# The messages of a graph layer by Strassen's product, four groups left out

## The chip, the cores and the metric

The kernel runs on one core of a Trainium2 chip. The core has a matrix engine (TensorE, PE in the profile; PEld is its loading of weights), a vector engine (VectorE, DVE), a scalar engine (ScalarE, ACT), a general engine (GpSimd, POOL) and an engine that issues most transfers (SyncE, SP). They work side by side, each on its own queue in order, and wait for one another by semaphores. TensorE writes its results to PSUM, eight banks of 128 x 512 fp32 numbers; the other engines read them from there into SBUF. The metric is the device time of one execution in microseconds (us).

## The reference: two layers on 128 graphs

The input is `x`, 128 graphs of 128 nodes with 256 features, and a sparse adjacency for each. Layer 0 mixes two projections by a gate and normalises. Layer 1, which the change touches, computes per graph (all in fp32):

```python
msg = relu(x @ w_msg.T + b_msg)                    # 128 nodes x 256
A = exp(-dist)                                     # from 3 coordinates per node
x_nmp = A @ msg                                    # over the nodes
x_in = concatenate([x_conv, x_nmp])                # x_conv: two convolutions over the nodes
gi = x_in @ w_ih.T + b_ih                          # 128 x 768
gh = x @ w_hh.T + b_hh                             # 128 x 768
r, z = sigmoid(gi_r + gh_r), sigmoid(gi_z + gh_z)
out = (1 - z) * tanh(gi_n + r * gh_n) + z * x
x = layernorm(x + out)
```

The second layer's adjacency multiplies `A` in the code in place of the mask (L974). The product of the change is the one in the first line: 128 nodes x 256 features by 256 x 256 weights, for each graph.

## The kernel before, in words

The work has three stages: layer 0 with the start of layer 1 over 64 pairs of graphs (to about 670 us), the convolution in the frequency domain (to 848 us), and a loop over 32 groups of G = 4 graphs for all the rest (848 us to the end). The change lies in the third stage.

What one group `g` goes through there:

- `load_c`, `load_x1`, `load_y` read its `x1T` (features on partitions, 256 x 512 nodes), adjacency, `x1` and convolution coefficients by SP's queue, two groups ahead.
- `l1_project(g)` makes the sums of `x1T` on POOL (`l1_sums`, tile `sh`) and the messages: for each pair of graphs a PSUM bank, in it for each graph two matmuls of 128 x 128 weights by 256 columns (L927). DVE adds the bias (L931, 128 x 512), ACT applies the relu (L935). Groups 2 and 3 (`EARLY`) got their messages in the first stage and only read them back.
- `l1_own`, `l1_kernel` make the distances of two groups at once in the tile `acc`, which holds four whole banks; ACT takes the exponential (L970), DVE multiplies the adjacency (L974).
- `l1_synth(d)` is the way back of the convolution for two groups, also in the four banks of `acc` (L891, L898); DVE adds `x1T` (L908), ACT applies the relu (L911), POOL makes the sums `sc`.
- `l1_gather(g)` multiplies `A` by the messages (`nmp_ps`, L983, eight matmuls of 128 columns); ACT copies (L987), DVE makes the sums `sm`.
- `l1_gru(g, pr)`, for each of the two pairs of graphs, makes the gates by Strassen's product in Winograd's form: the pair of graphs and the two halves of the features make a 2 x 2 block matrix, the weights another, and seven products take the place of eight. Each product is three matmuls of 384 columns (`g_ps`, L1050) into one bank of the pool `psC`, which has four banks, taken in turn. DVE adds the products up (L1063 to L1067, L1085, L1086) and so empties the banks; two of the additions are on POOL (L1083, L1084). `l1_update` finishes the gates (L1009 to L1025) and the norm (L308, L309, POOL's L192 and L193, L316, L318).

The left factors of a Strassen product are blocks of the input and four sums of them. `l1_sums` makes the four: s1 (L997), s2 (L998), s3 (L999), s4 (L1000), for `x1T` in `sh`, for the convolution in `sc`, for the gathered messages in `sm`. The right factors are blocks of the weights and four differences, made once in `l1_factors`.

TensorE's order in the loop is written out by hand: gather of `g`, messages of `g + 1`, first gates of `g`, and after odd `g` the way back of the next two groups, then second gates of `g`; after odd `g` the distances of the next two groups stand between the fourth and the fifth product of the second gates. A planner orders the other engines from the order of the program and the costs that it assumes. So three things are in turn in `acc` (and, with the change, four), and the four banks of `psC` go round among everything else.

An "even group" below is an even `g`, whose gather is followed by the messages of `g + 1`; before it TensorE had the distances, after an odd one comes the way back.

Of the kernel before, what the change touches and what calls it, by code (L numbers as in the profile page):

```python
# [9 lines left out]
F32 = mybir.dt.float32  # L10
I32 = mybir.dt.int32
AF = mybir.ActivationFunctionType
ALU = mybir.AluOpType

P = 128
D = 256
NC = D // P
J = 2
G = 4
# [15 lines left out]
def gnn_layers_kernel(ctx: ExitStack, tc: tile.TileContext, a: dict, out: bass.AP):  # L35
# [10 lines left out]
    nc = tc.nc  # L46
# [30 lines left out]
    w_msg = const.tile([P, NC, D], F32, tag="w_msg", name="w_msg")  # L77
    b_msg = const.tile([P, D], F32, tag="b_msg", name="b_msg")
# [244 lines left out]
    def nodes(q):  # L323
        return slice(q * P, (q + 1) * P)
# [366 lines left out]
    def cpool(name, bufs, stack=cctx, **kw):  # L691
        return stack.enter_context(tc.tile_pool(name=name, bufs=bufs, reuse_waits="tile", **kw))
# [91 lines left out]
    with tc.manual_schedule(engines={E.Activation, E.Pool}):  # L784
        for k in range(M // 2):
# [4 lines left out]
            for blk in range(2):  # L790
                for c in range(NC):
                    nc.tensor.matmul(  # L792
                        py[:, blk, :], lhsT=coefs(blk if k == 0 else 2 * k + 1 - blk, c),
                        rhs=w[:, blk, c, :], start=(c == 0), stop=(c == NC - 1),
# [3 lines left out]
            else:  # L798
# [5 lines left out]
                for c in range(NC):  # L804
                    nc.tensor.matmul(  # L805
                        pz[:, 0, :], lhsT=hs[:, c, :], rhs=ws[:, c, :],
                        start=(c == 0), stop=(c == NC - 1),
# [15 lines left out]
    ck = cpool("ck", 2)  # L823
    acc = cpool("acc", 1, space=PSUM)
    psc = cpool("psC", 4, space=PSUM)

    def bankc(name):
        return psc.tile([P, 512], F32, tag="ps", name=name)

    cs = cpool("cs", 1)  # L830
    factors = {}

    def l1_factors():

        for kind, w in (("h", w_hh), ("c", w_ih[:, 0:NC]), ("m", w_ih[:, NC : 2 * NC])):
            t = cs.tile([P, 4, 3 * P], F32, tag=f"t{kind}", name=f"t_{kind}")
            b11, b12, b21, b22 = (w[:, c, h, :] for c in range(NC) for h in range(2))
            nc.vector.tensor_sub(t[:, 0, :], b12, b11)
            nc.vector.tensor_sub(t[:, 1, :], b22, t[:, 0, :])
            nc.vector.tensor_sub(t[:, 2, :], b22, b12)  # L840
            nc.vector.tensor_sub(t[:, 3, :], t[:, 1, :], b21)
            factors[kind] = (b11, b21, b22, t[:, 3, :], t[:, 0, :], t[:, 1, :], t[:, 2, :])

    def load_c(g):
        s = st[g] = {}
        s["x1T"] = wb.tile([P, NC, 2, D], F32, tag="w", name=f"cx1T_{g}").rearrange("p c r o -> p c (r o)")
        for r in range(2):
            nc.sync.dma_start(s["x1T"][:, :, r * J * P : (r + 1) * J * P], x1T_d[2 * g + r])
        s["adjT"] = ci.tile([P, G, P], F32, tag="adjT", name=f"cadjT_{g}")
        nc.sync.dma_start(s["adjT"], adjT[:, g * G : (g + 1) * G, :])  # L850

    def load_x1(g):
        s = st[g]
        if g in EARLY:
            s["msg"] = ck.tile([P, G, D], F32, tag="msg", name=f"msg_{g}")
            for r in range(2):
                nc.sync.dma_start(
                    s["msg"][:, r * J : (r + 1) * J, :].rearrange("p j e -> p (j e)"),
                    msg_d[EP.index(2 * g + r)],
                )  # L860
        s["x1"] = ci.tile([P, G, D], F32, tag="x1", name=f"cx1_{g}")
        nc.sync.dma_start(
            s["x1"], x1_d[2 * g : 2 * g + 2].rearrange("r j n e -> n (r j) e")
        )
# [3 lines left out]
    def load_y(d):  # L868

        yl = cy.tile([P, P], F32, tag="yl", bufs=2, name=f"yl_{d}")  # L870
        for e in range(2):
            g = 2 * d + e
            yt = cy.tile([P, G, D], F32, tag="yt", name=f"yt_{g}")
            nc.sync.dma_start(yt, y_d[g * G : (g + 1) * G, 0:P, :].rearrange("q m f -> m q f"))
            for c in range(NC):
                r = NC * e + c
                nc.sync.dma_start(
                    yl[32 * r : 32 * r + 32],
                    y_d[g * G : (g + 1) * G, P:M, c * P : (c + 1) * P],
                )  # L880
            sy[g] = yt, yl


    def l1_synth(d):
        four = acc.tile([P, 4, 512], F32, tag="acc", name=f"conv2_ps_{d}")
        pcs = {}
        for e in range(2):
            for c in range(NC):
                pc = pcs[e, c] = four[:, NC * e + c, :]
                for q in range(G):  # L890
                    nc.tensor.matmul(  # L891
                        pc[:, nodes(q)], lhsT=sy[2 * d + e][0][:, q, c * P : (c + 1) * P], rhs=S,
                        start=(q == 0), stop=False, skip_group_check=True,
                    )
        for e in range(2):
            for c in range(NC):
                k = slice(32 * (NC * e + c), 32 * (NC * e + c) + 32)
                nc.tensor.matmul(  # L898
                    pcs[e, c], lhsT=sy[2 * d + e][1][k, :],
                    rhs=SLb[k].rearrange("p q n -> p (q n)"),  # L900
                    start=False, stop=True, skip_group_check=True,
                )
        for e in range(2):
            s = st[2 * d + e]
            s["xcT"] = ck.tile([P, NC, G * P], F32, tag="xcT", bufs=3, name=f"xcT_{2 * d + e}")
            for c in range(NC):
                dst = s["xcT"][:, c, :]
                nc.vector.scalar_tensor_tensor(  # L908
                    dst, pcs[e, c], scale2[:, c : c + 1], s["x1T"][:, c, :], ALU.mult, ALU.add
                )  # L910
                nc.scalar.activation(dst, dst, AF.Relu, bias=shift2[:, c : c + 1])  # L911
            l1_sums(2 * d + e, "c", s["xcT"], nc.gpsimd)


    def l1_project(g):
        s = st[g]
        x1T = s["x1T"]
        l1_sums(g, "h", x1T, nc.gpsimd)
        if g in EARLY:
            return  # L920
        msg = ck.tile([P, G, D], F32, tag="msg", name=f"msg_{g}")
        for pr in range(G // 2):
            pm = bankc(f"msg_ps_{g}_{pr}")
            for j in range(2):
                q = 2 * pr + j
                for c in range(NC):
                    nc.tensor.matmul(  # L927
                        pm[:, j * D : (j + 1) * D], lhsT=x1T[:, c, nodes(q)], rhs=w_msg[:, c, :],
                        start=(c == 0), stop=(c == NC - 1),
                    )  # L930
            nc.vector.tensor_tensor(  # L931
                msg[:, 2 * pr : 2 * pr + 2, :], pm.rearrange("p (j e) -> p j e", j=2),
                b_msg.unsqueeze(1).to_broadcast([P, 2, D]), ALU.add,
            )
        nc.scalar.activation(msg, msg, AF.Relu)  # L935
        s["msg"] = msg

# [53 lines left out]
    def l1_sums(g, kind, src, engine):  # L991

        v = src.rearrange("p c (r j n) -> p c r j n", r=G // 2, j=2)
        a11, a12, a21, a22 = (v[:, c, :, j, :] for j in range(2) for c in range(NC))
        t = ck.tile([P, 4, G // 2, P], F32, tag=f"s{kind}", name=f"s{kind}_{g}")
        s1, s2, s3, s4 = (t[:, i] for i in range(4))
        engine.tensor_tensor(s1, a21, a22, ALU.add)  # L997
        engine.tensor_tensor(s2, s1, a11, ALU.subtract)  # L998
        engine.tensor_tensor(s3, a11, a21, ALU.subtract)  # L999
        engine.tensor_tensor(s4, a12, s2, ALU.subtract)  # L1000
        st[g][f"f{kind}"] = (a11, a12, s4, a22, s1, s2, s3)
# [91 lines left out]
    with tc.manual_schedule(engines={mybir.EngineType.PE}):  # L1093
        load_c(0)
        load_c(1)
        load_y(0)
        for g in range(2):
            load_x1(g)
            l1_own(g)
        l1_project(0)  # L1100
        l1_kernel(0, 1)
        l1_project(1)
        l1_factors()
        l1_synth(0)
        for g in range(NG):
            d = g // 2
            if g + 2 < NG:
                load_c(g + 2)
                if g % 2 == 0:
                    load_y(d + 1)  # L1110
                load_x1(g + 2)
                l1_own(g + 2)
            l1_gather(g)
            if 2 <= g + 1 < NG:
                l1_project(g + 1)
            l1_gru(g, 0)
            if g % 2 == 1 and d + 1 < ND:
                l1_synth(d + 1)
            if g + 1 < NG:

                l1_gru(g, 1, {4: lambda: l1_kernel(g + 1, g + 2)} if g % 2 == 1 else {})
# [44 lines left out]
```

## Time and profile before

| | |
|---|---|
| time, median of 3 runs | 1989.94 us (1989.74 to 1992.71) |
| profiled execution, its own time | 1989.79 us |
| its span, first to last instruction | 1988.0 us |
| PE busy | 1948.1 us (98%) |
| PEld busy | 1322.5 us (67%) |
| DVE busy | 1452.2 us (73%) |
| ACT busy | 743.2 us (37%) |
| POOL busy | 701.0 us (35%) |
| messages on PE (L927), 480 instructions | 108.7 us |
| gates on PE (L1050) as a share of the chain that ended last | 43% |

An instruction's row shows its start, its duration, engine, line, what it writes and reads, and, in brackets, how long the engine had idled before it and for whom. Durations of successive instructions overlap, so the distance from start to start says what one costs its engine. A matmul of fp32 counts as two instructions. The third stage repeats itself every two groups, 70.36 us (`nmp_ps` of groups 18 and 20 start at 1484.68 and 1555.04).

### The profile page before, as it was taken

The numbers are of one execution on the slowest core, as the hardware profiler recorded it, in microseconds if no ns is written. First come the engines' busy times: TensorE is split into PE (matmuls) and PEld (weight loads), VectorE is DVE, ScalarE is ACT, GpSimd is POOL, SyncE is SP. The second block draws the span as 40 slices with busy tenths as digits, with TensorE's granted clock in tenths as the row PEclk, the third lists the DMA queues.
The fourth block names the chain that finished last, engine by engine and source line by source line (L and its number), as shares of the span: only waits on it lengthen the run. The fifth ranks groups of instructions, "written<-read, shape, count | busy, mean of one in ns | idle before, by whom it ended". The sixth has DMA issues, their size and how long they took to land.

```text
span 1988.0 us, 26049 instructions
## 1 busy us (share of the span) xinstructions
PE 1948.1 (98%) x8203; PEld 1322.5 (67%) x8203; DVE 1452.2 (73%) x2866; ACT 743.2 (37%) x1489; POOL 701.0 (35%) x983
## 2 busy tenths in 40 slices
PE   8999999999999999999999999999999999999996
PEld 5666666666666788866666666666666666666663
DVE  7788888888888544477677767777776776767775
ACT  3666666666665311122222222222232222222221
POOL 3223232232322355543333424323342433333331
PEclk9999999999999999999999999999999999999998
DMA  5787877777776799962212221221221222121100
GB/s 148 213 240 211 240 211 230 236 225 221 230 223 195 265 316 334 315 205 82 81 48 68 78 71 59 81 67 62 66 81 57 72 76 64 57 79 54 37 12 22
DMA packets 328687, 279.87 MB, mean 141 GB/s; under 512 B 150885, under 2 KB 268909, under 8 KB 328550
## 3 DMA queue, kind: packets, MB, share of 16 engines
q1 hardware_dynamic: 317622, 264.32, 43.1%
q0 software_dynamic: 4224, 8.37, 1.6%
q10 hardware_dynamic: 6704, 5.52, 0.9%
q8 instruction: 67, 1.10, 0.2%
q14 instruction: 70, 0.57, 0.1%
HBM read 173.26 MB, written 104.86 MB: 140 GB/s over the span
## 4 chain that ended last, share of the span: by engine, by line
PE 64%; DVE 1%; DMA 0%; issue 0%; ACT 0%; POOL 0%; POOLq 0%; ACTq 0%; SPq 0%; DVEq 0%
PE g_ps L1050 43%; PE y_ps L792 5%; PE msg_ps L927 5%; PE nmp_ps L983 3%; PE conv_ps L891 3%; PE z_ps L805 3%; PE conv_ps L898 1%; PE dist_ps L964 1%; DMA wb<-w_d 0%; ACT o L1009 0%; DVE hs L802 0%; PE turn_ps L943 0%; DVE coords L725 0%; DVE o L1019 0%; DVE left L727 0%
## 5 line engine op out<-in xcount | busy, mean ns | idle before, releaser
L353 PE MATMUL f_ps<-w,xT 128*128 128x512 f32 x512 | 246.2, 603 | 8.5 <-DVE xT L423 6.9
L192 POOL TENSOR_SCALAR rstd_b<-mv_b 128x2 f32<-128x2 f32 (+1 forms) x65 | 12.5, 192 | 529.8 <-DVE mv_b L309 529.8
L1009 ACT ACTIVATE o<-o 128x1024 f32<-128x1024 f32 (+1 forms) x65 | 67.8, 1044 | 268.8 <-DVE o L1086 264.8
L353 PEld LDWEIGHTS f_ps<-w,xT 128*128 128x128 f32 x512 | 89.5, 190 | 110.2 <-issue 77.7
L1050 PE MATMUL g_ps<-t_h,sh 128*128 128x384 f32 x384 | 156.8, 490 | 0.0
L1050 PE MATMUL g_ps<-t_c,sc 128*128 128x384 f32 x384 | 155.2, 486 | 0.0
L1050 PE MATMUL g_ps<-t_m,sm 128*128 128x384 f32 x384 | 155.2, 486 | 0.0
L318 ACT ACTIVATE y<-y,nb_b,rstd_b 128x256 f32<-128x256 f32 x128 | 70.0, 593 | 219.0 <-DVE nb_b L316 219.0
L358 PEld LDWEIGHTS gate_ps<-w,xT 128*128 128x128 f32 x512 | 97.4, 190 | 68.1 <-issue 53.9
L1083 POOL TENSOR_TENSOR u<-u,p 128x512 f32<-128x512 f32 x63 | 79.8, 1267 | 162.6 <-DVE p L1067 162.6
L358 PE MATMUL gate_ps<-w,xT 128*128 128x256 f32 x512 | 131.4, 379 | 0.0
L792 PE MATMUL y_ps<-wb,H 128*128 128x256 f32 x544 | 128.4, 379 | 0.8 <-POOL ws L800 0.8
L445 PE MATMUL conv_ps<-conv_w,x1T 128*128 128x259 f32 x512 | 122.8, 382 | 5.5 <-DVE x1T L423 3.7
L800 POOL TENSOR_TENSOR ws<-wb 128x512 f32<-128x512 f32 x67 | 93.3, 1392 | 91.9 <-PE z_ps L805 54.7
L192 POOL TENSOR_SCALAR rstd_a<-mv_a 128x2 f32<-128x2 f32 x64 | 12.2, 191 | 299.9 <-DVE mv_a L309 238.9
L362 ACT ACTIVATE hom<-f_ps,norm 128x256 f32<-128x256 f32 x128 | 60.6, 473 | 145.7 <-PE f_ps L353 139.2
L792 PEld LDWEIGHTS y_ps<-wb,H 128*128 128x128 f32 x544 | 103.2, 190 | 15.1 <-POOL ws L800 1.0
L445 PEld LDWEIGHTS conv_ps<-conv_w,x1T 128*128 128x128 f32 x512 | 96.8, 190 | 21.8 <-issue 4.9
L927 PE MATMUL msg_ps<-w_msg,cx1T 128*128 128x256 f32 x480 | 108.7, 379 | 0.0
L1050 PEld LDWEIGHTS g_ps<-t_c,sc 128*128 128x128 f32 x384 | 73.0, 190 | 50.9
L1050 PEld LDWEIGHTS g_ps<-t_m,sm 128*128 128x128 f32 x384 | 73.0, 190 | 50.9
L1050 PE MATMUL g_ps<-w_hhT_w,cx1T 128*128 128x384 f32 x256 | 105.1, 492 | 0.0
(220 smaller groups left out, 4441.2 us busy)
## 6 DMA issues: line engine op xcount, KB each, us to landing
wb<-w_d SPq DMA_DIRECT2D x68, 512.0 KB
w_d<-w_o SPq DMA_DIRECT2D x32, 1024.0 KB
y_d<-yb SPq DMA_DIRECT2D x68, 256.0 KB
x<-in_x SPq DMA_DIRECT2D x64, 256.0 KB
x_d<-x SPq DMA_DIRECT2D x64, 256.0 KB
cx1T<-x1T_d SPq DMA_DIRECT2D x64, 256.0 KB
yt<-y_d SPq DMA_DIRECT2D x32, 512.0 KB
cx<-x_d SPq DMA_DIRECT2D x32, 512.0 KB
```

What stands on the lines that cost most here:

```text
L318: nc.scalar.activation(dst[:, q, :], src[:, q, :], AF.Identity, bias=nb[:, q : q + 1], scale=rstd[:, q : q + 1],)
L353: nc.tensor.matmul(pf, lhsT=xT[:, c, nodes(j)], rhs=w0[:, c, 0 : 2 * D], start=(c == 0), stop=(c == NC - 1),)
L358: nc.tensor.matmul(pg[:, j * D : (j + 1) * D], lhsT=xT[:, c, nodes(j)], rhs=w0[:, c, 2 * D : 3 * D], start=(c == 0), stop=(c == NC - 1),)
L362: nc.scalar.activation(hom[:, j, :], pf[:, 0:D], AF.Copy, scale=norm[:, j : j + 1])
L445: nc.tensor.matmul(ph[:, 0 : D + CO], lhsT=s["x1T"][:, c, nodes(j)], rhs=conv1_w[:, c, :], start=(c == 0), stop=(c == NC - 1),)
L792: nc.tensor.matmul(py[:, blk, :], lhsT=coefs(blk if k == 0 else 2 * k + 1 - blk, c), rhs=w[:, blk, c, :], start=(c == 0), stop=(c == NC - 1),)
L800: nc.gpsimd.tensor_tensor(ws, w[:, 0], w[:, 1], ALU.add)
L805: nc.tensor.matmul(pz[:, 0, :], lhsT=hs[:, c, :], rhs=ws[:, c, :], start=(c == 0), stop=(c == NC - 1),)
L927: nc.tensor.matmul(pm[:, j * D : (j + 1) * D], lhsT=x1T[:, c, nodes(q)], rhs=w_msg[:, c, :], start=(c == 0), stop=(c == NC - 1),)
L1009: nc.scalar.activation(rz, rz, AF.Tanh, scale=0.5)
L1050: nc.tensor.matmul(pg[:, lo : lo + 3 * P], lhsT=s[f"f{kind}"][i][:, pr, :], rhs=factors[kind][i], start=(k == 0), stop=(k == 2), skip_grou ...
L1083: nc.gpsimd.tensor_tensor(u4, u2, p5, add)
```

## The change

Groups 0 and 1 keep their messages as they were (`g < 2`), groups 2 and 3 still read theirs back. For the 28 groups from 4 on, the two graphs of a pair and the two halves of the features make the same 2 x 2 blocks as in the gates. Seven products of 128 columns are made for each pair, with left factors `s["fh"]`, the blocks and sums of `x1T` that the gates use too, and right factors from `w_msg`, made once in the new `l1_msg_factors`, which also subtracts the first half of the bias from the second. The products of both pairs lie side by side in `acc`, in half banks, in the order 0, 5, 1, 6, 4, 3, 2; number 5 uses s2, 6 s3, 4 s1 and 2, the last, s4. In place of two additions of 128 x 512 on DVE there are seven of 128 x 256 on DVE, each reading PSUM, and two on POOL, the second of the seven outputs (`o12`) going from DVE to POOL and back to DVE.

```diff
+    def l1_msg_factors():
+
+        t = cs.tile([P, 4, P], F32, tag="tg", name="t_g")
+        b11, b12, b21, b22 = (w_msg[:, c, h * P : (h + 1) * P] for c in range(NC) for h in range(2))
+        nc.vector.tensor_sub(t[:, 0, :], b12, b11)
+        nc.vector.tensor_sub(t[:, 1, :], b22, t[:, 0, :])
+        nc.vector.tensor_sub(t[:, 2, :], b22, b12)
+        nc.vector.tensor_sub(t[:, 3, :], t[:, 1, :], b21)
+        factors["g"] = (b11, b21, b22, t[:, 3, :], t[:, 0, :], t[:, 1, :], t[:, 2, :])
+        nc.vector.tensor_sub(b_msg[:, P:], b_msg[:, P:], b_msg[:, 0:P])
...
         msg = ck.tile([P, G, D], F32, tag="msg", name=f"msg_{g}")
-        for pr in range(G // 2):
-            pm = bankc(f"msg_ps_{g}_{pr}")
...
+        if g < 2:
+            for pr in range(G // 2):
+                pm = bankc(f"msg_ps_{g}_{pr}")
...
+        else:
+            four = acc.tile([P, 4, 512], F32, tag="acc", name=f"msg_ps_{g}")
+            made = {}
+            for at, i in enumerate((0, 5, 1, 6, 4, 3, 2)):
+                pm = four[:, at // 2, at % 2 * D : (at % 2 + 1) * D]
+                for pr in range(G // 2):
                     nc.tensor.matmul(
-                        pm[:, j * D : (j + 1) * D], lhsT=x1T[:, c, nodes(q)], rhs=w_msg[:, c, :],
-                        start=(c == 0), stop=(c == NC - 1),
+                        pm[:, pr * P : (pr + 1) * P], lhsT=s["fh"][i][:, pr, :], rhs=factors["g"][i],
+                        start=True, stop=True, skip_group_check=True,
                     )
-            nc.vector.tensor_tensor(
-                msg[:, 2 * pr : 2 * pr + 2, :], pm.rearrange("p (j e) -> p j e", j=2),
-                b_msg.unsqueeze(1).to_broadcast([P, 2, D]), ALU.add,
+                made[i] = pm.rearrange("p (r e) -> p r e", r=G // 2)
+            v, add, sub = nc.vector, ALU.add, ALU.subtract
+            m = msg.rearrange("p (r j) (h e) -> p j h r e", j=2, h=2)
+            o11, o12, o21, o22 = (m[:, j, h] for j in range(2) for h in range(2))
+            p5 = ck.tile([P, G // 2, P], F32, tag="mp5", bufs=1, name=f"mp5_{g}")
+            b1, b2 = (
+                b_msg[:, h * P : (h + 1) * P].unsqueeze(1).to_broadcast([P, G // 2, P]) for h in range(2)
             )
+            v.tensor_tensor(o11, made[0], b1, add)
+            v.tensor_tensor(o12, made[5], o11, add)
+            v.tensor_tensor(o11, made[1], o11, add)
+            v.tensor_tensor(o22, made[6], o12, add)
+            v.tensor_tensor(p5, made[4], b2, add)
+            v.tensor_tensor(o21, o22, made[3], sub)
+            nc.gpsimd.tensor_tensor(o12, o12, p5, add)
+            nc.gpsimd.tensor_tensor(o22, o22, p5, add)
+            v.tensor_tensor(o12, made[2], o12, add)
         nc.scalar.activation(msg, msg, AF.Relu)
...
         l1_factors()
+        l1_msg_factors()
         l1_synth(0)
```

The built program shows what the planner makes of this. On POOL the sums `sh` keep their place, behind L1084's addition of the group before, and after an even group s4 stays behind three of the `sc` sums; the two new additions come behind `rstd` of the norm. On DVE the seven new additions come between L1021 and the first eviction of the gates, L1063 (lines of the kernel before), the last one directly ahead of it; the norm's statistics and `nb` (L308, L309, L316), which stood behind that eviction or mixed with it, now stand ahead of it too.

## The prediction

> **What bounds the kernel now.** First the table by stage: busy time of each engine in the third stage, the loop over the 32 groups. Columns: the window, its length, then busy time of PE, PEld, DVE, ACT and POOL with instruction counts, granted clock, DMA share, GB/s.
>
> ```profile
> 880.00:1940.00 1060.00, 1060.00 (x4337) 691.00 (x4336) 763.66 (x1390) 286.19 (x428) 397.49 (x484) 1.00 0.21 65
> ```
>
> TensorE is busy in every microsecond of this stage; VectorE (DVE) 72%, GpSimd (POOL) 37%. So a shorter message step is worth what it takes off TensorE, provided that nothing makes TensorE wait. The chain of work that ended last gives the lengths (start, us, what):
>
> ```profile
> 1555.20 1.78 PE nmp_ps L983 x16
> 1556.99 3.46 PE msg_ps L927 x16
> 1560.44 27.09 PE g_ps L1050 x84
> ```
>
> Each fp32 matmul is two instructions. Sixteen with 128 columns follow each other in 1.78 us (0.111 each), though each has new weights; sixteen with 256 in 3.46 (0.216); a gate product of six takes 27.09 / 14 = 1.935. Time is columns here; a weight load (190 ns in its row) hides.
>
> Next I look for slack around one message step, in the timelines. I count from E, the start of the `nmp_ps` matmuls: 1555.04 for an even group here.
>
> ```profile
> 1555.04 1.95 PE L983 MATMUL nmp_ps<-AT,msg 128*128 128x128 f32 x16
> ...
> 1568.02 0.81 PE L1050 MATMUL g_ps<-t_h,sh 128*128 128x384 f32 x2
> ```
>
> The second row is the fifth gate product, at E+12.98. The pool psC has four banks and the products take them in turn, so the fifth needs the bank of the first, which DVE empties at L1063 (`u1`). GpSimd's queue, with the sums `sh` for the next group:
>
> ```profile
> 1553.91 1.26 POOL L1084 TENSOR_TENSOR o<-u,p 128x512 f32<-128x512 f32 x1
> ...
> 1556.51 0.72 POOL L998 TENSOR_TENSOR sh<-sh,cx1T 128x256 f32<-128x256 f32 x1
> ...
> 1559.89 1.17 POOL L1000 TENSOR_TENSOR sh<-cx1T,sh 128x256 f32<-128x256 f32 x1
> ...
> 1567.99 0.70 POOL L193 TENSOR_TENSOR rstd_b<-rstd_b,neg_half 128x2 f32<-128x2 f32 x1
> ```
>
> L998 is s2, done at E+2.19; L1000 is s4, done at E+6.02, behind three `sc` sums. And DVE's queue:
>
> ```profile
> 1557.20 1.27 DVE L1013 SCALAR_TENSOR_TENSOR o<-o 128x512 f32<-128x512 f32 x1 [1.20 <-ACT o L1009]
> ...
> 1560.40 0.95 DVE L997 TENSOR_TENSOR sm<-nmpT 128x256 f32<-128x256 f32 x1
> 1561.27 0.68 DVE L931 TENSOR_TENSOR msg<-msg_ps,b_msg 128x512 f32<-128x512 f32 x1
> 1561.87 0.68 DVE L1019 TENSOR_TENSOR o<-cx,o 128x512 f32<-128x512 f32 x1
> 1562.47 0.41 DVE L998 TENSOR_TENSOR sm<-sm,nmpT 128x256 f32<-128x256 f32 x1
> 1562.81 0.68 DVE L1021 SCALAR_TENSOR_TENSOR o<-o 128x512 f32<-128x512 f32 x1
> ...
> 1564.34 0.68 DVE L931 TENSOR_TENSOR msg<-msg_ps,b_msg 128x512 f32<-128x512 f32 x1
> 1564.94 0.67 DVE L1025 TENSOR_TENSOR y<-o,cx 128x512 f32<-128x512 f32 x1
> 1565.54 0.68 DVE L1063 TENSOR_TENSOR u<-g_ps,bias 128x512 f32<-128x512 f32 x1
> 1566.14 0.74 DVE L308 BATCH_NORM_STATS2 stats_b<-y 128x6 f32<-128x256 f32 x2
> ...
> 1567.46 0.17 DVE L309 BATCH_NORM_AGGREGATE mv_b<-stats_b 128x2 f32<-128x6 f32 x1
> 1568.73 0.16 DVE L316 SCALAR_TENSOR_TENSOR nb_b<-mv_b,rstd_b 128x2 f32<-128x2 f32 x1 [1.10 <-POOL rstd_b L193]
> ```
>
> DVE is the late one: from the end of a group until u1 it hardly rests (E+2.16 to E+10.50), starting from one instruction to the next in 0.60 us at 128x512 and 0.34 at 128x256. u1 ends at E+11.18, so the slack before the fifth product is only 1.80 us here, and the same 1.8 to 2.0 after every other even group, 3.2 after odd ones (u1 at E+9.09). It is the number on which the change turns.
>
> **The change part by part.** It touches 28 steps (messages of groups 4 to 31): 14 follow an even group's `nmp_ps`, 14 an odd one's.
>
> *TensorE's own work.* 16 instructions of 256 columns become 28 of 128: 3.46 us becomes 28 x 0.111 = 3.12, or -0.34 per step, -9.6 in all. A rule of the Trainium skill speaks against this: "TensorE: Matmul & The Clock Gate", section "Back-to-back issue gap", has the spacing in a stream of weight loads and matmuls set by both, 81 ns at 128 columns and 131 at 512. On a straight line between them 256 columns are 98 ns, so 28 x 81 against 16 x 98 is a step 1.45 times as long, 5.0 us instead of 3.46 (an estimate by that page). With that estimate the fifth product after an odd group would start at 1.78+5.0+4 x 1.935 = E+14.5 instead of the 13.15 found below, 14 x 1.37 = 19 us more, and the total would be near 2035 us. The rows here halve with the columns, so I take -0.34.
>
> *The wait for s2 and s4.* The messages now read `sh`. Product two needs s2, at E+1.78+0.45 = E+2.23: after an even group it is there, after an odd one it ends at E+2.54 (wait 0.3). The last product needs s4 at E+1.78+6/7 x 3.12 = E+4.45; after an even group s4 ends at E+5.41 to E+6.02, so TensorE stands 1.0 to 1.6 us there. In the changed program's order POOL still has the `sh` sums behind L1084's add and s4 behind three `sc` sums, so nothing moves them. Behind that wait stand the gate products: their start goes from E+5.24 to E+5.9 or E+6.5.
>
> *The evictions, and what they hold up.* DVE loses two adds of 128x512 (1.20 us) and gains seven of 128x256, reading PSUM. Such an operation by itself is not in this loop; I take 0.34 from the `sm` rows, and the lower end 0.30 is half of a 128x512 one, the upper 0.42 the duration of the 128x256 PSUM add at L449 (422 ns). More important is the order in the changed program: all seven stand ahead of u1, and so do the norm's statistics, which came after it, `nb` with its wait for `rstd` from POOL, and the last add, which waits for POOL's new add to o12. That POOL add stands behind `rstd`. Step by step from E=1555.04:
> - L1013, s3, L1015, s1 as the rows show them, to E+6.23. s2 of `sm`, now next, runs beside POOL's last `sc` sum: 0.70 (0.75 between starts in the window at 1490.41), to 6.93. Then L1019 7.53, s4 7.87, L1021 8.47.
> - add 1 to 8.81, L1023 9.41, add 2 9.75, L1025 10.35, add 3 10.69, the two statistics (0.66) 11.35, first aggregate 11.43, add 4 11.77, second aggregate 11.85, add 5 (p5) 12.19.
> - `nb` starts 1.27 after the second aggregate (1567.46 to 1568.73): 11.77+1.27 = 13.04, to 13.12. Add 6 to 13.46.
> - POOL ends `rstd` 1.23 after that aggregate, 13.00; its add to o12 at 128x256 takes 0.73 (row 0.72; beside DVE 1.18, the upper end): 13.73. Add 7 starts 13.76, to 14.10.
> - u1 starts 14.10 instead of 10.50, ends 14.78; the fifth product starts 14.83 instead of 12.98: **+1.85**. The 0.34 saved and the wait for s4 are both inside this, since DVE is later than either.
>
> Where the transposed coordinates are made just before E (six of the 14 even groups), L1021 starts at E+7.42 instead of 7.87 (1492.10 less 1484.68): +1.40. For the last (group 30) u1 was at 10.10, 0.40 earlier: +1.45. After an odd group there are no `sc` sums on POOL: s1 ends at E+4.82, s2 5.16, L1019 after its tanh 5.85, s4 6.19, which is 1.68 before 7.87, so the fifth product is at E+13.15: +0.17.
>
> *Edits I cost at nothing.* The five new subtractions of `l1_msg_factors` (128x128, about 1 us) stand before the evictions of the first way back, where DVE idled 0.42 us; the first gate product to use that result started 0.81 us after its relu ended (861.66+0.72 to 863.19). Both together cover them; without either they would cost their 1 us once. POOL's second add ends near E+14.5, its next work (u4) comes after E+18. ScalarE's relu waits for it until then, and the next in its queue is the tanh at E+20; the message is read 32 us after E. The acc tile was emptied 6.5 us before the message products take it, and its next user, the way back at E+18.8 after an odd group, comes 6 us after the last message read. No DMA is added or moved: SP's queue stays. psC loses two turns per group, which is counted in the walk.
>
> *Sum.* 6 x 1.40 + 7 x 1.85 + 1.45 + 14 x 0.17 = 8.4 + 13.0 + 1.5 + 2.4 = **+25.2 us**. The profiled execution took 1989.79 us (span 1988.0), 0.15 under the median of 1989.94, so about **2015 us**. Bounds of the open costs: adds at 0.30 take 28 x 0.28 = 7.8 off at most (odd steps can give back only 0.5), near 2010; adds at 0.42 give +0.56 and a POOL add at 1.18 another +0.45 per step, +28 in all, 2043.
>
> **The rivals.**
> 1. *Faster: neither wait binds.* All that is left is -9.6: 1980. For it, s4 must end before E+4.45 and u1 must end before E+12.6; the rows and the order say 5.4 to 6.0 and 13.1 to 14.8. It decides if DVE comes to u1 about 2 us sooner than my walk. Chance 0.05.
> 2. *Only the sums bind*, DVE being quicker at the small adds, or the bank wait elsewhere. The gate products then start 0.45 after s4: 6 x 0.67 + 7 x 1.28 + 0.88 + 14 x 0.02 = +14: 2004. Against it: u1 needs no slow add to be late, its place in the queue is enough. Chance 0.13.
> 3. *Contention:* the upper ends above, 2043. For it: L1013 goes from 0.69 to 1.27 beside POOL's sums; against it: the new adds read PSUM, and L1085 keeps 0.69 beside POOL. Chance 0.15.
> 4. *The two effects cancel:* within 0.2% (4 us, about what a measurement of this kernel can tell from no change). It would need a walk 20 us off. Chance 0.01.
>
> **How the numbers follow.** My forecast has 0.66 (spread 2006 to 2030). The range from just below rival 2 to two thirds of the way to rival 3 is 2003 to 2036. Rival 1 alone is faster, rival 4 the same: faster 0.05, same 0.01, slower 0.94.
>
> **What would show it.** Right: TensorE stops being gapless; about 1.4 to 1.8 us are lost before each fifth gate product's bank after even groups, split with a wait of 1.0 to 1.6 for POOL's `sh` inside the message products, and hardly any after odd ones; the message's instructions run at 0.111; u1 near E+14 and E+12.5; DVE waits twice for POOL (`rstd`, then the last message add). The period of two groups grows from 70.4 by about 1.8 us. Wrong: gaps at the way back or the distances instead, or a gapless TensorE.

## The result and the profile after

The change makes the kernel slower: median 2025.54 us (2024.16 to 2028.94, 5 runs) against 1990.87 us (1989.74 to 1992.71, 5 runs), ratio 1.0170 with a 95% interval of 1.0157 to 1.0183. The profiled execution took 2025.42 us (span 2023.6). From the `nmp_ps` matmuls of group 3 to those of group 31, between which all 28 changed steps lie, the trace before has 986.27 us and the trace after 1020.71: +34.44. (This stretch is called the loop from here on.) The two profiled executions differ by 35.6; the 1.1 that remain stand before group 0. In the execution after, the clock was at half for 3.4 us near 651 us, in the one before it was not. The forecast, which put the whole change into the loop, was +25.2.

From the page of the changed kernel, the busy times and the shares of the chain that ended last:

```profile
PE 1957.3 (97%) x8539; PEld 1327.3 (66%) x8539; DVE 1506.1 (74%) x3011; ACT 743.7 (37%) x1489; POOL 742.2 (37%) x1039
...
PE 45%; DVE 15%; POOL 2%; ACT 2%; issue 2%; DMA 0%; ACTq 0%; POOLq 0%; DVEq 0%
```

In the chain PE had 64% and DVE 1% before. The chain, followed back from the end, now leaves TensorE again and again and goes through VectorE, from which it waits for a bank. The waits of the changed kernel (engine, what it would write, for whom; us in all, how often, the longest):

```profile
PEld g_ps L1089 <- DVE u L1102: 26.5, 28, 1.2
...
PE msg_ps L953 <- POOL sh L1039: 15.3, 14, 1.3
PE g_ps L1089 <- DVE u L1102: 8.6, 14, 0.6
```

L1102 is u1, the eviction at L1063 before; L1039 is the sum s4. Both waits that the prediction named are there. TensorE's matmuls stand at each of them after the 14 even groups; after the 14 odd ones the loading of weights (PEld) waits for u1 too, and the fifth product starts only 0.05 us after the matmul before it has ended. The order of one step, group 20, in TensorE's timeline (start, us, what, idle before; E = 1576.38):

```profile
1576.38 1.95 PE L1022 MATMUL nmp_ps<-AT,msg 128*128 128x128 f32 x16
...
1578.16 0.61 PE L953 MATMUL msg_ps<-w_msg,cx1T 128*128 128x128 f32 x4
...
1580.52 0.61 PE L953 MATMUL msg_ps<-t_g,cx1T 128*128 128x128 f32 x4
...
1582.45 0.71 PE L953 MATMUL msg_ps<-w_msg,sh 128*128 128x128 f32 x4 [1.32 <-POOL sh L1039]
1583.00 0.81 PE L1089 MATMUL g_ps<-w_hhT_w,cx1T 128*128 128x384 f32 x2
...
1591.52 0.91 PE L1089 MATMUL g_ps<-t_h,sh 128*128 128x384 f32 x2 [0.61 <-DVE u L1102]
1592.27 0.81 PE L1089 MATMUL g_ps<-t_c,sc 128*128 128x384 f32 x2
```

The last message product waits 1.32 us for s4, so the gates begin at E+6.62 instead of E+5.24; the fifth gate product then waits another 0.61 for its bank and begins at E+15.14 instead of E+12.98. Note the last two rows: the first pair after a wait takes 0.75 from start to start, where the unwaited pairs take 0.645. Each wait costs this 0.1 besides. It also costs 0.16 more than its brackets say: they count from the end of the record before, 0.81 after its start, and without a wait the next pair would have begun at 0.645.

VectorE in the same step:

```profile
1588.26 0.16 DVE L309 BATCH_NORM_AGGREGATE mv_b<-stats_b 128x2 f32<-128x6 f32 x1
1588.35 0.38 DVE L969 TENSOR_TENSOR mp<-msg_ps,b_msg 128x256 f32<-128x256 f32 x1
1589.53 0.68 DVE L316 SCALAR_TENSOR_TENSOR nb_b<-mv_b,rstd_b 128x2 f32<-128x2 f32 x1 [0.80 <-POOL rstd_b L193]
1590.13 0.41 DVE L970 TENSOR_TENSOR msg<-msg,msg_ps 128x256 f32<-128x256 f32 x1
1590.46 0.41 DVE L973 TENSOR_TENSOR msg<-msg_ps,msg 128x256 f32<-128x256 f32 x1
1590.79 0.67 DVE L1102 TENSOR_TENSOR u<-g_ps,bias 128x512 f32<-128x512 f32 x1
```

and GpSimd beside it:

```profile
1581.22 1.17 POOL L1039 TENSOR_TENSOR sh<-cx1T,sh 128x256 f32<-128x256 f32 x1
...
1588.79 0.70 POOL L193 TENSOR_TENSOR rstd_b<-rstd_b,neg_half 128x2 f32<-128x2 f32 x1
1589.46 0.73 POOL L971 TENSOR_TENSOR msg<-msg,mp 128x256 f32<-128x256 f32 x1
1590.61 0.73 POOL L972 TENSOR_TENSOR msg<-msg,mp 128x256 f32<-128x256 f32 x1 [0.43 <-DVE msg L970]
```

u1 starts at E+14.41 (10.50 before). What was not in the forecast stands in the row of L316, `nb`: it works on two numbers per partition and took 0.16 us before; now 0.68. It ends at 1590.21, just after POOL's new addition L971 (1589.46 to 1590.19), which starts in the moment that `rstd` is done, that is, always together with `nb`.

By kind of step, predicted and measured (E is the start of `nmp_ps`; before, the fifth product was at E+12.98 everywhere):

| step | how many | fifth product, predicted | measured | growth of the step, predicted | measured |
|---|---|---|---|---|---|
| after an even group | 7 | 14.83 | 15.14 | 1.85 | 2.27 |
| the same, with turned (transposed) coordinates made just before E | 6 | 14.38 | 14.55 | 1.40 | 1.67 |
| group 30 | 1 | 14.43 | 14.75 | 1.45 | 1.87 |
| after an odd group | 14 | 13.15 | 13.34 | 0.17 | 0.46 |

7 x 2.27 + 6 x 1.67 + 1.87 + 14 x 0.46 = 34.2; the step of group 9, which grew by 0.74 and not by 0.46, brings it to the 34.4 of the loop, within rounding. In every row the excess is that of the fifth product plus the 0.10 that TensorE loses after its wait.

### The profile page after: what moved, and what is told of

Read it like the earlier page. It is cut to its first block, busy times and chain, and to the rows that moved or that the text cites. A ratio compares the mean times of both kernels' runs of the same rounds, so it can differ in the third digit from the quotient of the medians.

```text
span 2023.6 us, 26894 instructions
## 1 busy us (share of the span) xinstructions
PE 1957.3 (97%) x8539; PEld 1327.3 (66%) x8539; DVE 1506.1 (74%) x3011; ACT 743.7 (37%) x1489; POOL 742.2 (37%) x1039
## 4 chain that ended last, share of the span: by engine, by line
PE 45%; DVE 15%; POOL 2%; ACT 2%; issue 2%; DMA 0%; ACTq 0%; POOLq 0%; DVEq 0%
PE g_ps L1089 31%; PE y_ps L792 6%; PE conv_ps L902 3%; PE z_ps L805 3%; ACT o L1048 2%; DVE o L1052 1%; DVE o L1054 1%; POOL rstd_b L193 1%; DVE o L1125 1%; DVE sm L1038 1%; DVE stats_b L308 1%; DVE o L1058 1%; DVE o L1060 1%; DVE y L1064 1%; DVE u L1102 1%
## 5 line engine op out<-in xcount | busy, mean ns | idle before, releaser
L1089 PEld LDWEIGHTS g_ps<-t_h,sh 128*128 128x128 f32 x384 | 69.4, 189 | 67.8 <-DVE u L1102 26.5
L1052 DVE SCALAR_TENSOR_TENSOR o<-o 128x512 f32<-128x512 f32 (+1 forms) x65 | 54.1, 832 | 69.5 <-ACT o L1048 69.5
```

The costliest lines, as they stand in the source:

```text
L1052: v.scalar_tensor_tensor(gh, r, 1.0, gh, add, ALU.mult)
L1089: nc.tensor.matmul(pg[:, lo : lo + 3 * P], lhsT=s[f"f{kind}"][i][:, pr, :], rhs=factors[kind][i], start=(k == 0), stop=(k == 2), skip_grou ...
```

## The experiments

The theory: TensorE loses time by two waits in a row, s4 inside the messages and u1 before the fifth gate product; u1 is the later one and sets the time, since all of the message's evictions, the norm's statistics and `nb` with its waits stand ahead of it on DVE. The rivals: the sums alone set it; it is contention, that is, operations which have grown longer; the small matmuls cost more than the rows of before said.

### Sums one group sooner

```diff
-        l1_sums(g, "h", x1T, nc.gpsimd)
+        if g < 4:
+            l1_sums(g, "h", x1T, nc.gpsimd)
...
             l1_gru(g, 0)
+            if 4 <= g + 2 < NG:
+                l1_sums(g + 2, "h", st[g + 2]["x1T"], nc.gpsimd)
...
-        t = ck.tile([P, 4, G // 2, P], F32, tag=f"s{kind}", ...)
+        t = ck.tile([P, 4, G // 2, P], F32, tag=f"s{kind}", bufs=3 if kind == "h" else 2, ...)
```

The tile of the turned coordinates goes down to one buffer, to make room.

> The sums sh of a group are made one group sooner (after the first gates of two groups before, a third buffer for them, one buffer fewer for the turned coordinates), all else as in the changed kernel. Theory (the fifth gate product waits for u1, which stands late in DVE's queue, and the wait for the sums lies inside that wait): the waits of the message products for sh (15.3 us on PE) vanish and those for u1 grow by as much; the time stays within 3 us of the changed kernel's 2025.5. Rival (the sums carry the loss): the 14 to 16 us of those waits come off, about 2010.

Measured: 2032.76 us (2031.77 to 2033.69), ratio to the kernel before 1.0210 [1.0195, 1.0226]; the loop takes 1027.14. The waits for `sh` are gone and the gates begin at E+4.91 in every step, as meant; the fifth product stays at E+15.14 (even), 14.54 (turned) and 13.33 (odd). So in these 27 steps TensorE's wait for the sums did not set the end: u1 did. The 28th, group 30, is different. GpSimd has no sums of `x1T` to make there; VectorE's sums `sm` (L1039, L1037) take 0.41 us instead of 0.94, its gate operation between them (L1055) 0.68 instead of 1.21, and u1 comes at E+12.13 instead of 14.02. So the sums cost time by running beside VectorE, and in the other steps this edit leaves them where they did that. But the time went up by 7 us, where I had expected at most 3. Its timeline and its windows (length, busy time of PE, PEld, DVE, ACT, POOL, then granted clock, DMA share, GB/s):

```profile
1598.34 1.65 PE L1090 MATMUL g_ps<-t_h,sh 128*128 128x384 f32 x2 [2.33 <-DVE u L1103]
1599.78 1.49 PE L1090 MATMUL g_ps<-t_c,sc 128*128 128x384 f32 x2
...
1602.01 0.81 PE L1090 MATMUL g_ps<-t_h,cx1T 128*128 128x384 f32 x2
```

```profile
1598.40:1602.00 3.60, 3.60 (x6) 1.98 (x7) 1.97 (x3) 0.85 (x1) 0.00 (x0) 0.55 0.24 77
1602.00:1610.00 8.00, 8.00 (x26) 4.75 (x25) 4.01 (x7) 1.08 (x2) 2.49 (x2) 1.00 0.00 0
```

What had been two waits, 1.32 and 0.61 with 8 us of matmuls between them, is now one of 2.33. Right after it the clock is granted at half for 3.4 us: a pair takes 1.4 instead of 0.645. It happens five times in the loop, and such a step is 36.3 long instead of 34.6. Five times 1.7 is 8.5, less 1.9 for the step of group 30: the 6.4 us by which the loop is longer, within rounding. No part of my theory said this.

### The message's evictions behind the first gates

```diff
-            v.tensor_tensor(o11, made[0], b1, add)
-            ...
-        nc.scalar.activation(msg, msg, AF.Relu)
+            def evict():
+                v.tensor_tensor(o11, made[0], b1, add)
+                ...
+                nc.scalar.activation(msg, msg, AF.Relu)
+            s["evict"] = evict
...
-            l1_gru(g, 0)
+            l1_gru(g, 0, {4: lambda: st[g + 1].pop("evict")()} if "evict" in st.get(g + 1, {}) else {})
```

> The seven additions of the messages, the two on POOL and the relu stand in the program at the fifth product of the first gates, so that u1 and the norm's statistics keep the places that they had before the change; the sums sh stay where they are. Theory: no wait for u1 is left; what is left is the start of the first gates, which the profile of the changed kernel shows late by 0.77 us at six steps, 1.38 at seven, 0.98 at one and 0.14 at fourteen, 17 us together: about 2008. Rival (the sums carry nothing, only the adds do): 1982. Rival (the order on DVE carries nothing): 2025.

Measured: 2009.44 us (2006.88 to 2010.24), ratio 1.0095 [1.0078, 1.0112]; loop 1004.08. u1 is on time again (E+10.50 in group 20), the fifth product has no wait of its own, and what is left is the sums'. In the waits of this kernel:

```profile
PE msg_ps L953 <- POOL sh L1045: 15.4, 14, 1.5
...
PE msg_ps L953 <- POOL sh L1043: 3.0, 14, 0.5
```

This is rival 2 of the prediction made on purpose. It was priced there at +14 and measures +17.8 in the loop. In most steps the gates begin some 0.1 later than in that price, since the first instructions after a wait are slower (0.55 for the message's last four instead of 0.45 in the rows above); 28 x 0.1 is 2.8 of the difference. Three steps are 0.3 to 0.4 longer still (groups 8, 9 and 18), and group 30's is 0.35 shorter than its price.

### Both

The two edits together.

> The sums one group sooner and the additions later, the two edits before together. Theory: no wait is left, and what remains is the matmuls' own saving, 3.46 less 3.14 us at 28 steps, 9 us: about 1982, faster than the kernel before. Rival (28 loads of weights instead of 16 cost more than the columns save once nothing else hides it): 1991 or more.

Measured: **1984.03 us** (1982.62 to 1985.89), ratio **0.9965 [0.9952, 0.9978]**: faster than both kernels. The loop takes 977.13, which is 9.1 less than before. TensorE's timeline in group 20 (E = 1552.86):

```profile
1552.86 1.95 PE L1029 MATMUL nmp_ps<-AT,msg 128*128 128x128 f32 x16
1554.65 0.61 PE L954 MATMUL msg_ps<-w_msg,cx1T 128*128 128x128 f32 x4
...
1557.33 0.61 PE L954 MATMUL msg_ps<-w_msg,sh 128*128 128x128 f32 x4
1557.77 0.81 PE L1096 MATMUL g_ps<-w_hhT_w,cx1T 128*128 128x384 f32 x2
...
1565.52 0.81 PE L1096 MATMUL g_ps<-t_h,sh 128*128 128x384 f32 x2
```

No row has an idle time in brackets. The 28 small matmuls go from 1554.65 to 1557.77, 3.12 us or 0.111 each, and the steps are 32.01 and 37.69 to 37.91 long instead of 32.33 and 38.02 to 38.24. The windows of this kernel, and after them those of the changed one, over 1000 us of the loop:

```profile
900.00:1900.00 1000.00, 1000.00 (x4474) 660.62 (x4473) 759.42 (x1457) 274.35 (x410) 415.19 (x513) 1.00 0.21 67
```

```profile
900.00:1900.00 1000.00, 974.17 (x4281) 633.91 (x4280) 748.65 (x1401) 261.90 (x392) 399.70 (x494) 1.00 0.22 66
```

TensorE has no gap in the one and misses 25.8 us in the other, and that with the same arithmetic. Of the 9.1 us, 2.2 are given back between group 0 and group 3. There is one new wait there, before the first gates of group 0:

```profile
866.25 0.91 PE L1096 MATMUL g_ps<-w_ihT_w,xcT 128*128 128x384 f32 x2 [1.71 <-ACT xcT L922]
```

Every kernel with the early sums has it; it is taken up again below.

### Without POOL's two additions

```diff
-            nc.gpsimd.tensor_tensor(o12, o12, p5, add)
-            nc.gpsimd.tensor_tensor(o22, o22, p5, add)
```

> The two additions of the messages on POOL are left out (the second product block is missing from two of the four outputs, so the numbers are not the reference's); DVE's order stays. Theory (POOL's first addition starts in the moment in which nb starts on DVE and holds it up, 0.68 us instead of 0.16, and this is why the change cost 9 us more than the sum of the prediction): u1 comes 0.52 us sooner at 28 steps, 14.6 us off, about 2011. Rival (the excess is TensorE's restart after each wait, or the longer additions): within 2 us of 2025.5.

Measured: 2012.58 us (2012.31 to 2016.06), ratio 1.0113 [1.0098, 1.0128]; loop 1008.67. The timeline of VectorE:

```profile
1581.10 0.16 DVE L316 SCALAR_TENSOR_TENSOR nb_b<-mv_b,rstd_b 128x2 f32<-128x2 f32 x1 [0.79 <-POOL rstd_b L193]
1581.18 0.41 DVE L970 TENSOR_TENSOR msg<-msg,msg_ps 128x256 f32<-128x256 f32 x1
1581.51 0.42 DVE L971 TENSOR_TENSOR msg<-msg_ps,msg 128x256 f32<-128x256 f32 x1
1581.85 0.68 DVE L1100 TENSOR_TENSOR u<-g_ps,bias 128x512 f32<-128x512 f32 x1
```

`nb` is back at 0.16 and gives way after 0.08; u1 is 0.52 sooner (E+13.89 after an even group, 14.41 with the additions), and the fifth product is at 14.62, 0.2 before the forecast. These 13 us hang on POOL's additions, and the 0.52 is what `nb` had been held. The 14.6 of the theory were not reached: after odd groups the step gets only 0.31 shorter, because there the fifth product no longer waits (E+13.11) before the 0.52 are used up.

### Early sums, without POOL's additions

> The sums one group sooner as in e1 and the two additions on POOL left out as in e4 (the second product block is missing from two of the four outputs). In e1 the single wait for u1 was 2.33 us after seven even groups, and five times the granted clock fell to half for 3.4 us right after it; in the changed kernel the same time was lost in two waits of 1.32 and 0.62 with the clock at full. Here the single wait should be 2.33 less 0.5, some 1.8 to 2.0 us. Theory (the length of one wait brings the half clock, 1.7 us each): no such stretch in the loop, and the sum of e4 less 0.31 at fourteen steps and 1.5 at the last, about 2007. Rival (the sums one group sooner cost by their new place on POOL or DVE): the 7 to 8 us that e1 had over the changed kernel stay, about 2014 to 2020, with the clock at full.

Measured: 2011.25 us (2009.03 to 2014.29), ratio 1.0101 [1.0086, 1.0116]; loop 1004.27, 4.4 shorter than without the early sums. Here one wait of TensorE is 1.82 us long (1.22 with turned coordinates), and the clock stays whole in the loop. The time lies between the theory's 2007 and the rival's 2014, and decides little; the trace does: no step has a slow clock. Of the 4 us over 2007, 2.2 are the wait before the first gates of group 0, and 1.5 are the steps after odd groups, which gave 0.20 each instead of 0.31.

### POOL's two additions on VectorE

```diff
-            nc.gpsimd.tensor_tensor(o12, o12, p5, add)
-            nc.gpsimd.tensor_tensor(o22, o22, p5, add)
+            v.tensor_tensor(o12, o12, p5, add)
+            v.tensor_tensor(o22, o22, p5, add)
```

> As the changed kernel, but the two additions on POOL are on DVE, in the same place of the order. Theory (POOL's first addition holds nb up for 0.52 us; two more additions cost DVE 0.34 each): nb back to 0.16 us, u1 later by 0.16 us at 28 steps, about 2030. Rival (it is the trip to POOL and back that costs): under 2020.

Measured: 2028.77 us (2026.88 to 2030.07), ratio 1.0187 [1.0170, 1.0204]; loop 1024.51. In the timeline of VectorE:

```profile
1590.86 0.16 DVE L316 SCALAR_TENSOR_TENSOR nb_b<-mv_b,rstd_b 128x2 f32<-128x2 f32 x1 [0.79 <-POOL rstd_b L193]
```

`nb` is short without anything being left out, so it was POOL's addition beside it that held it. But the two additions now stand in DVE's own queue ahead of u1 (E+14.56, 0.15 later), so nothing is won: here the place in the queue counts, not the engine that adds.

### The wait in group 0

In the kernel with both edits the third buffer lets POOL make the sums of group 2 before the loop, from 853.7 to 857.8 us, while DVE makes the factors of the gates. Here they are held back until the gathered sums of group 0 are there.

```diff
-        if g < 4:
+        if g < 2:
             l1_sums(g, "h", x1T, nc.gpsimd)
...
-            if 4 <= g + 2 < NG:
+            if g + 2 < NG:
                 l1_sums(g + 2, "h", st[g + 2]["x1T"], nc.gpsimd)
...
+        if kind == "h" and g == 2:
+            for t_ in (s1, s3):
+                engine.tensor_tensor(t_, st[0]["fm"][4], st[0]["fm"][4], ALU.add)
```

> As e3, but the sums of x1T of group 2 cannot start before the gathered sums of group 0 are there (two more additions on POOL write two of the four sums first, from those; they are then overwritten). In e3 POOL made them from 853.7 to 857.8 us, beside DVE's subtractions for the gate factors, and three of those took 1.08 us instead of 0.55 and the adjacency product 1.81 instead of 1.29 for two: 2.1 us by which DVE came later to the way back, and TensorE stood 1.71 us before the first gates of group 0. Theory (POOL's sums hold DVE there): the subtractions are back at 0.55, the wait of 1.71 is gone, the loop after group 3 is as in e3 (977), and the time is 1984.0 less 2.2 = 1981.8. Rival (the third buffer or the earlier loads are the cause): the wait stays and the time is 1984.

Measured: 1983.84 us (1981.26 to 1986.01), ratio 0.9962 [0.9949, 0.9974]; loop 977.13. VectorE and TensorE in the timelines:

```profile
854.88 0.55 DVE L840 TENSOR_TENSOR t_h<-w_hhT_w 128x384 f32<-128x384 f32 x1
855.34 0.55 DVE L841 TENSOR_TENSOR t_h<-t_h,w_hhT_w 128x384 f32<-128x384 f32 x1
856.91 0.56 DVE L838 TENSOR_TENSOR t_c<-w_ihT_w 128x384 f32<-128x384 f32 x1 [1.02 <-DMA yt<-y_d]
```

```profile
866.03 0.91 PE L1099 MATMUL g_ps<-w_ihT_w,xcT 128*128 128x384 f32 x2 [0.69 <-ACT xcT L922]
```

The subtractions are back at 0.55 (1.08 in the kernel with both edits), and TensorE's wait falls from 1.71 to 0.69; the stretch from group 0 to group 3 falls from 94.84 to 93.82, where it is 92.65 before. So POOL's sums were about half of it, 1.02 of 2.19. The rest comes with an idle 1.02 us of DVE that the profile puts down to a transfer of the stage before; that the third buffer has moved `t_c` to a place which this transfer frees is my guess, and was not tried. The expected 1981.8 was not reached, and the medians can't show the 1 us.

### Early sums, POOL's additions on VectorE

> As e1, with POOL's two additions on DVE as in e6, which brought DVE to its first eviction 0.14 us later. The wait of TensorE before the fifth product should be 2.4 to 2.5 us after even groups (7 of them) and 1.8 to 1.9 where the coordinates are turned (6). Theory (the length of the one wait brings the half clock): stretches of half clock of 3.4 us again after the long waits, five to seven of them in the loop, none after the short, and 2033 to 2037 us. Rival (the half clock of e1 has to do with what POOL does beside DVE in that wait): none, and about 2033 + 2 - 8.5 = 2026 us.

Measured: 2047.51 us (2047.24 to 2051.58), ratio 1.0288 [1.0273, 1.0304], above the 2033 to 2037 of the theory; loop 1041.40, 14.3 more than with the early sums alone. TensorE's timeline in group 20 and in group 22:

```profile
1606.90 0.91 PE L1090 MATMUL g_ps<-t_h,sh 128*128 128x384 f32 x2 [2.49 <-DVE u L1103]
1607.65 1.35 PE L1090 MATMUL g_ps<-t_c,sc 128*128 128x384 f32 x2
1608.80 1.49 PE L1090 MATMUL g_ps<-t_m,sm 128*128 128x384 f32 x2
...
1681.60 0.91 PE L1090 MATMUL g_ps<-t_h,sh 128*128 128x384 f32 x2 [1.88 <-DVE u L1103]
1682.35 0.97 PE L1090 MATMUL g_ps<-t_c,sc 128*128 128x384 f32 x2
1683.11 1.49 PE L1090 MATMUL g_ps<-t_m,sm 128*128 128x384 f32 x2
```

The half clock follows all seven waits of 2.48, and four of the six of 1.88, where I had expected none. The waits are 0.15 longer than with the early sums (28 x 0.15 = 4.2), and there are six more stretches of half clock (6 x 1.7 = 10.2): together 14.4, the 14.3 within rounding. So the length of a wait does not decide it by itself; the last section goes on with this. The rival, that the half clock has to do with POOL's work beside the wait, falls: without that work it comes more often.

## Why the prediction was right, and where it was off

- **The outcome and the mechanism: right.** Slower, inside the range of 2003 to 2036, and by the wait that was named: u1, behind all of the message's evictions, the statistics and `nb`. Its price is shown by the second experiment: with the evictions out of its way 16 us are won back. That the wait for s4 (1.32 measured, 1.0 to 1.6 forecast) is inside u1's and not added to it is shown by the first: without it the fifth product starts at the same place (in all steps but group 30's).
- **The size: 34.4 instead of 25.2.** The term that was mis-sized is "`nb` starts 1.27 after the second aggregate ..., to 13.12", with 0.08 from start to start. It measured 0.60, since POOL's new addition begins when `rstd` ends and runs beside it (0.68 against 0.16 with that addition taken away or moved). Working against it, the last addition did not have to wait for POOL: the 0.30 of "Add 7 starts 13.76" fell away, as `nb` had already waited out POOL's addition. In group 20 `nb` also started 0.11 later than in the walk (E+13.15); 0.52 - 0.30 + 0.11 is the 0.3 by which the fifth product came late. Without POOL's additions the walk is 0.2 too long rather than 0.3 too short. The contention was foreseen as a rival, but at the wrong instruction: I had put it on POOL's addition (1.18; it took 0.73). The range's upper end, 2036, is three quarters of the way from 2015 to rival 3's 2043 and not the two thirds of the text; 2025.5 is inside with either.
- **Left out: the restart.** After each wait TensorE's first pair takes 0.75 instead of 0.645. 28 x 0.10 = 2.8 of the missing 9.2.
- **TensorE's own work: right.** -0.34 a step and -9.6 in all were taken from rows that halve with the columns; with both waits gone the steps are 0.32 shorter and the loop 9.1. The rule in the Trainium skill, "TensorE: Matmul & The Clock Gate", section "Back-to-back issue gap", by which the estimate for the small matmuls came to 1.45 times the time of the large ones, does not hold for these fp32 matmuls: 28 of them take 3.12 us against 3.46 for the 16.
- **The rivals.** Rival 1 (1980) was the price of the change with neither wait; the kernel with both edits took 1984.0, most of the difference being the 2.2 us between group 0 and group 3, the 9.1 for 9.6, and 1.0 by which the kernel before was slower in these runs (1990.96) than in those of the forecast. Rival 2 (2004) took 2009.4 when it was built.

## What to carry to other kernels

A cheaper product on the engine that bounds a kernel is worth what it saves if its evictions do not queue ahead of the one that this engine waits for (here -9.1 us in the loop with them behind it and the sums early, +34.4 with them ahead): walk the queue of the evicting engine up to the instruction that frees the next bank, and move the new work behind it. When two waits lie one behind the other, removing the first alone wins nothing, as the second takes its time over, and it may lose, since the idle time is then in one piece; remove the later first. And look at what a new instruction on GpSimd runs beside: here an addition of 0.73 us held the shortest instruction of VectorE until it was done.

## What the hardware showed that was not expected

**The clock after a wait of 2 us.** In these single-core executions a wait of TensorE in the loop was followed by 3.413 us at half clock in 16 of 39 cases that are longer than 1 us, in the three kernels with early sums and a late u1:

| kernel | wait, us | followed by half clock |
|---|---|---|
| early sums, additions on VectorE | 2.48 | 7 of 7 |
| early sums | 2.33 | 5 of 7 |
| early sums, additions on VectorE | 1.88 | 4 of 6 |
| early sums, no additions | 1.82 | 0 of 7 |
| early sums | 1.72 | 0 of 6 |
| early sums, no additions | 1.22 | 0 of 6 |

Length alone does not decide it; where it lies seems to decide the rest. In each trace the starts of these stretches are whole multiples of 3.413 us apart (71.680 + 3.413 = 75.093 us, or 22 of them, most often). If I lay this grid over the loop, 0.08 us earlier than the clock's records, every wait that had at least 1.88 us inside one interval of the grid was followed by the half clock in the next, and every one that had at most 1.85 there was not, all 39 of them. The shift was fitted to get this (0.06 to 0.15 will do for these 39), but other waits can test it. From 40 us on to the end of the loop the ten traces of this case have 75 more waits of over 1 us. All ten have one of about 2 us near 650 us, where the half clock followed in four, each with at least 1.91 inside one interval, and not in the six with at most 1.85. Of all 75 one does not fit: in the kernel with early sums a wait from 656.07 to 658.01 had 1.92 in one interval and the clock stayed whole. So the limit is near 1.9 us in these traces, and what exactly is counted stays open. The changed kernel's own waits of 1.32 and 0.61, 8 us apart, stay below it, and its clock is whole throughout the loop.

The Trainium skill, "TensorE: Matmul & The Clock Gate", Part 1, section "What's actually happening", has a free-running window of 3413 ns by which the clock is granted; the stretches here are of that length and on such a grid. It gives an idle window of about 3.4 us as what halves the clock, and there these runs differ: about 1.9 us of idling inside one window were enough.

**One instruction held by another engine.** A 128x2 operation of VectorE takes 0.16 us alone and 0.68 beside an addition of 128x256 on GpSimd; in the kernel with both edits three subtractions of 128x384 in SBUF take 1.08 each beside GpSimd's sums, instead of 0.55. The Trainium skill, "SBUF — State Buffer", section "Who interferes with whom", says that an instruction of VectorE with two inputs from SBUF contends with one of GpSimd that reads SBUF, and that the order of issue decides which of them is held. These rows agree: both kinds have two inputs from SBUF, while u1, which reads one of its two from PSUM, keeps its 0.67 beside GpSimd's second addition (L972) in the rows of the changed kernel.
